# Two cross-attention and expert layers: token lists, maxima in seven pieces, and an opening in order of use

## The chip, the cores and the metric

The kernel runs on one core of one Trainium2 chip. The metric is the device time of one launch in microseconds (us); the median of several runs counts. The profiled execution is one launch taken by the hardware profiler.

A short glossary for the profile: PE is TensorE (matmuls), PEld its weight loads, DVE is VectorE, ACT is ScalarE, POOL is GpSimd, SP is SyncE (here it only issues transfers). L735 is line 735 of the kernel. Every engine works through its own queue of instructions in order and waits on semaphores where data of another engine is needed.

## The reference

Four layers are added to x in turn (4 batches of 512 tokens, 256 wide); ctx_1024 holds 1601 context tokens a batch.

```python
x = x + L0_xattn(ctx_1024, layernorm(x), ...)   # 8 heads of 128, keys: 512 latents + 1601 context
x = x + L0_ffn(layernorm(x), ...)               # 8 experts, top 2, capacity 512 each, tanh gelu
x = x + L1_xattn(ctx_1024, layernorm(x), ...)   # 8 heads of 32, keys: 1601 context
x = x + L1_ffn(layernorm(x), ...)               # 8 experts, top 2, no capacity, exact gelu
```

In the first attention the latents are normalized a second time, queries come from the latents, keys and values from latents and context together, and every score row goes through a softmax over 2113 keys. The last layer is, per token, a softmax over its top two router logits (and ties with the second), and the weighted sum of these experts:

```python
logits = xf @ Wr + br
thresh = lax.top_k(logits, 2)[0][:, 1:2]
weights = softmax(where(logits >= thresh, logits, -inf), axis=-1)
h = gelu(einsum('td,edh->eth', xf, W1) + b1[:, None, :])
out = einsum('etd,te->td', einsum('eth,ehd->etd', h, W2) + b2[:, None, :], weights)
```

## The kernel before

All is float32, in tiles of 128 partitions. A scheduler places the instructions on the engines by the order of the program and by what they depend on; inside a block `in_order` fixes the order of the program on the named engines. The stages follow one another.

**First attention** (lines 529 to 899; profile to about 1640 us). The opening loads x, the constants, the context of batch 0 and the weights (`load_ctx`, 562; the loads stand at 546 to 582), normalizes the context by all 13 tiles at once and the latents twice (`keys_input`, 584), turns both and writes them into `kvin`, whose layout is 17 blocks of 4 x 32 positions (`group`, 607). The output bias is summed by eight matmuls, each with a weight tile that DVE fills (801). `queries_keys` (661) makes one head's queries and keys; each of its five key steps (681) takes 512 neighbouring positions of `kvin`, of all four quarters, so that it needs the whole context. Then 128 steps follow, each one head and 128 queries: `scores` (729) puts 128 x 2113 scores into the single five-bank buffer `ps_s`, DVE takes the maximum (743), ACT the exp (749), and `exchange` (752) moves the result between partitions by 16 transfers, 12 issued by SP and 4 by ACT; one step later DVE turns it (764), and from step 3 on PE weighs the values (772). `attn` has two buffers, so the exp of step n+2 waits for the exchange of step n. Work for later steps is put into `later[n]`.

Before the first step two things are issued: `clear_rows` (370), which fills the DRAM tables `rows_a` (2048 rows) and `rows_b` (18688 rows) of 265 numbers each with an empty row, from SP; and `clear_slots` (178), which clears the slots of the first expert layer, from POOL.

**First expert layer** (to about 1940 us): per expert 512 slots, then the results are gathered again.

**Second attention** (lines 1056 to 1373; 1940 to 2665 us): 16 units (batch, half of the heads, half of the queries) of 13 key tiles. For each unit the row maxima are needed beforehand: `maxima` (1122) is called eight times for the next unit while this one runs; a call makes four matmuls of 400 keys into two buffers of `ps_s` (three buffers of two banks in all, which `weights` shares) and two reductions on DVE (1141). `negated` and `to_row` (1148, 1159) put the negative maximum into an extra row of the queries. `weights` (1173) makes the scores of one key tile and their exp; `add_weights` (1196) sums the exps, on POOL for the tiles in `by_pool`, else on DVE; `weigh` (1204) multiplies with the values. The loop takes two key tiles a step: maxima, two `weights`, further maxima, then sums and weighing of the tiles of the step before. Beside it, at fixed steps, stand routing of the last layer (`route2`, 382) and keys and values of later batches.

`route2` normalizes and routes a batch. It builds `pay`, for each token 256 numbers, its own number as a float, and 8 weights, and POOL scatters these rows to `rows_a` (at most 256 rows an expert from the first three batches) and `rows_b` (the rest), 521.

**Second expert layer** (lines 1379 to 1694): first eight tiles of 256 rows, one for each expert, from `rows_a` (`first_tile`, 1402, SP loads them straight); then 13 tiles from `rows_b` (`further_tile`, 1566: POOL gathers rows and weights). `told` (1388) casts the token's number in a row to an integer, `to`; `turned` (1427), `hidden` (1437) and `second` (1459) compute; `add_out` (1475) adds the result to the output with a POOL scatter by `to`. Rows without a token have the number 65536, which the scatter leaves out.

## Time and profile before

| what | us |
|---|---|
| time, median of 3 runs (3011.76 to 3015.57) | 3014.13 |
| the profiled execution | 3014.63 |
| its span, first to last instruction | 3012.6 |
| mean granted TensorE clock | 0.965 |
| busy: DVE / ACT / POOL | 1444.5 / 931.1 / 473.7 |
| first maximum of the first attention starts | 57.07 |
| L743 maximum (128 of them), each | 2.36 |
| L749 exp (128), each | 2.02 |
| L1141 maxima reduction (256), each | 0.98 |
| L1477 scatter to the output on POOL (42), each | 1.58 |

The 4 MB for the slots and 21.5 MB for the rows are written by the clears: 36 transfers of 530 KB and one of 265 KB to `rows_b`, 4 of 530 KB to `rows_a`, 8 of 512 KB to the slots. The span is read by stretches: where TensorE's busy time equals the stretch and its clock is 1.00, only its own work counts; elsewhere one looks for what it waits for. "Idle before" in a group of instructions is the time in which the engine had nothing to do just before them, with the instruction or transfer that ended it.

### The profile page before, as it was taken

The page shows a single profiled execution, that of the slowest core. Times are in us where ns is not written, and L with a number is a line of the kernel's source. Part 1 is how long each engine was busy: PE and PEld are TensorE (multiplying, and loading weights), DVE is VectorE, ACT ScalarE, POOL GpSimd, SP SyncE. Part 2 cuts the span into 40 slices and gives each one's busy share as a digit, 9 for nine tenths or more (in the row PEclk, how much of TensorE's full clock was granted, in tenths as well). Part 3 has the DMA queues.
Part 4 walks back from the last instruction along what each step waited for, and adds up shares of the span by engine and source line. Part 5 has one row for each costly group of instructions (what it writes and reads, how often), then busy time and mean ns, then how long its engine had stood idle before and what let it go on. Part 6 is the DMA issues. An engine that isn't in the chain of part 4 may idle for free. (4 is left out here: it accounts for less than half of the span.)

```text
span 3012.6 us, 35574 instructions
## 1 busy us (share of the span) xinstructions
PE 2781.7 (92%) x13426; PEld 1846.2 (61%) x13426; DVE 1444.5 (48%) x2324; ACT 931.1 (31%) x1312; POOL 473.7 (16%) x340
## 2 busy tenths in 40 slices
PE   5699999999999999999997999788988888898998
PEld 2466676666666667666665566544444444467887
DVE  4256447554476444464444100177775757751110
ACT  2233234232343333332321212123433434341221
POOL 1000000100001000010000100122424434343442
PEclk9899999999999999999998999889999999999999
DMA  8743334433343333333334233210101110045652
GB/s 297 234 123 94 99 92 105 112 96 92 94 113 104 98 86 95 93 102 97 92 96 148 93 98 105 66 27 14 30 26 36 30 35 22 13 172 165 193 171 73
DMA packets 165103, 295.95 MB, mean 98 GB/s; under 512 B 43287, under 2 KB 81752, under 8 KB 161848
## 3 DMA queue, kind: packets, MB, share of 16 engines
q1 hardware_dynamic: 124024, 204.45, 24.2%
q0 software_dynamic: 16320, 53.42, 5.9%
q10 hardware_dynamic: 24576, 35.68, 4.6%
q8 instruction: 109, 1.79, 0.3%
q14 instruction: 74, 0.61, 0.1%
HBM read 97.86 MB, written 49.76 MB: 49 GB/s over the span
## 5 line engine op out<-in xcount | busy, mean ns | idle before, releaser
L743 DVE TENSOR_REDUCE top<-ps_s 128x1 f32<-128x2113 f32 x128 | 301.8, 2358 | 578.9 <-PE ps_s L735 578.9
L772 PE MATMUL ps_o<-pT,v 128*128 128x256 f32 x2176 | 520.9, 381 | 7.8 <-DVE pT L764 7.8
L735 PE MATMUL ps_s<-kT,qT 128*128 128x512 f32 (+1 forms) x1280 | 489.0, 527 | 26.7 <-ACT attn L749 26.3
L772 PEld LDWEIGHTS ps_o<-pT,v 128*128 128x128 f32 x2176 | 410.9, 191 | 124.8 <-issue 69.9
L735 PEld LDWEIGHTS ps_s<-kT,qT 128*128 128x128 f32 x1280 | 241.5, 191 | 276.3 <-issue 239.9
L749 ACT ACTIVATE attn<-ps_s,top 128x2113 f32<-128x2113 f32 x128 | 258.9, 2023 | 486.1 <-DVE top L743 411.5
L764 DVE STREAM_TRANSPOSE pT<-swapped 128x2176 f32<-128x2176 f32 x128 | 312.4, 2441 | 70.2 <-DMA swapped<-attn 59.4
L1141 DVE TENSOR_REDUCE tops<-ps_s 128x2 f32<-128x800 f32 (+1 forms) x256 | 241.0, 984 | 150.7 <-PE ps_s L1133 150.6
L1180 PE MATMUL ps_w<-asked,keyed 64*128 64x256 f32 (+1 forms) x1664 | 243.7, 418 | 45.7 <-DVE tops L1141 39.4
L685 PE MATMUL ps_k<-kvin,wkv 128*128 128x512 f32 (+1 forms) x640 | 261.9, 533 | 5.2 <-ACT kT L692 5.2
L718 PE MATMUL ps_v<-wkv,kvin 128*128 128x256 f32 x1088 | 253.5, 381 | 0.0
L1202 POOL TENSOR_TENSOR sum<-sum,pT 128x1024 f32<-128x1024 f32 x80 | 197.0, 2463 | 334.4 <-ACT pT L1193 243.5
L1180 PEld LDWEIGHTS ps_w<-asked,keyed 64*128 64x128 f32 (+1 forms) x1664 | 150.4, 193 | 155.6 <-DVE tops L1141 79.7
L1193 ACT ACTIVATE pT<-ps_w 128x1024 f32<-128x1024 f32 (+1 forms) x176 | 178.2, 1023 | 195.4 <-PE ps_w L1180 191.8
L718 PEld LDWEIGHTS ps_v<-wkv,kvin 128*128 128x128 f32 x1088 | 204.9, 190 | 32.7 <-issue 3.4
L692 ACT ACTIVATE kT<-ps_k,bqk 128x512 f32<-128x512 f32 (+1 forms) x160 | 97.1, 620 | 268.1 <-DMA swapped<-attn 128.8
L685 PEld LDWEIGHTS ps_k<-kvin,wkv 128*128 128x128 f32 x640 | 116.5, 192 | 81.0 <-issue 67.1
L1202 DVE TENSOR_TENSOR sum<-sum,pT 128x1024 f32<-128x1024 f32 x96 | 153.3, 1597 | 6.2 <-ACT pT L1193 3.0
L725 ACT COPY v<-ps_v 128x512 f32<-128x512 f32 x144 | 79.8, 560 | 226.2 <-PE ps_v L718 154.0
L1445 PE MATMUL ps_h<-xT,w_e 128*128 128x256 f32 x640 | 143.7, 383 | 3.7 <-issue 3.7
L1133 PE MATMUL ps_s<-kT,qT 32*128 32x400 f32 (+1 forms) x1024 | 142.1, 582 | 3.2 <-ACT pT L1193 2.6
L1464 PE MATMUL ps_y<-w_e,hT 128*128 128x256 f32 x640 | 144.4, 385 | 0.0
(261 smaller groups left out, 2635.6 us busy)
## 6 DMA issues: line engine op xcount, KB each, us to landing
swapped<-attn SPq DMA_DIRECT2D x1536, 68.0 KB
swapped<-attn ACTq DMA_DIRECT2D x512, 68.0 KB
rows_b<-empty SPq DMA_DIRECT2D x36, 530.0 KB
w<-in_w_dram SPq DMA_DIRECT2D x16, 1024.0 KB
w_e<-in_wall_dram SPq DMA_DIRECT2D x7, 2052.0 KB
cT<-in_ctxT_dram SPq DMA_DIRECT2D x4, 1601.0 KB
keyed<-kT SPq DMA_DIRECT2D x32, 200.1 KB
ctx_b<-in_ctx_dram SPq DMA_DIRECT2D x4, 1536.0 KB
```

What stands on the lines that cost most here:

```text
L685: nc.tensor.matmul(ps[:, :n], lhsT=wkv[:, c, hs], rhs=flat_kvin[c][:, j0 : j0 + n], start=c == 0, stop=c == DC - 1,)
L718: nc.tensor.matmul(ps[:, k, :], lhsT=flat_kvin[c][:, j * P : (j + 1) * P], rhs=wkv[:, c, cols], start=c == 0, stop=c == DC - 1,)
L735: nc.tensor.matmul(flat[:, j0 : j0 + n], lhsT=qT[:, t * P : (t + 1) * P], rhs=kT[:, j0 : j0 + n], start=True, stop=True,)
L743: nc.vector.tensor_reduce(top, flat[:, :L], AX.X, ALU.max, negate=True)
L749: nc.scalar.activation(attn[:, :L], flat[:, :L], AF.Exp, bias=top, accum_out=total)
L764: nc.vector.transpose(pT[:, :, k * P : (k + 1) * P].rearrange("p c (a i) -> p a c i", a=4), swapped.rearrange("p a (c i) -> p a c i", i=32),)
L772: nc.tensor.matmul(ps, lhsT=v[:, j - parts[part][0], (h % 2) * DH0 : (h % 2 + 1) * DH0], rhs=pT[:, j, :], start=j == 0, stop=j == NB - 1,)
L1141: nc.vector.tensor_reduce(tops[u][:, t, 2 * pair : 2 * pair + 2, k], pss[pair][:, :, : hi - lo], AX.X, ALU.max,)
L1180: nc.tensor.matmul(ps[:r, s, pair * QH : (pair + 1) * QH], lhsT=keyed[o][64 * s : 64 * s + 64, pair, j * P : j * P + r], rhs=asked[u % 3][ ...
L1193: nc.scalar.activation(pT[:r], ps[:r], AF.Exp)
L1202: (nc.gpsimd if k else nc.vector).tensor_tensor(to, to, pT[:r], ALU.add)
L1464: nc.tensor.matmul(ps, lhsT=hT[:, f, r * P : (r + 1) * P], rhs=w(WB1 + f * D, D), start=f == 0, stop=f == FC - 1,)
```

## The change

Three parts, in one diff.

Token lists: `rows_a` and `rows_b` now hold one row per token in the order of the tokens, written by one plain transfer each for a batch, and one zero row at the end. What is scattered are token numbers of 4 bytes, into `list_a` and `list_b`, which are filled with the number of the zero row at first (`clear_lists`). A tile of the last layer reads its list (`listed`, from SP for the first eight tiles, by a POOL gather for the others), then gathers its rows by it on POOL (`fetched`); the list itself is `to` for the scatter to the output. The slots are cleared by SP, one of eight transfers every second step from step 4 on, out of one zeroed tile.

Opening: loads are issued in an order written out, the context in groups of four tiles, the weights of head 0 before the rest. Context statistics and scaling go by four tiles (`first`), scaling on ACT; latents, statistics, turns, queries and keys of head 0 are interleaved in a fixed order. A key step now takes one quarter of the positions (and a fifth step the last block). The output bias goes to step 13.

Second attention: maxima come in seven pieces, six of 512 keys and one with the last 65 keys of both query tiles; they stand between the two key tiles of a step, and `by_pool` has four tiles in place of six, the first of which only starts POOL's sum.

```diff
-ROWS = E * PLACES
+LIST = E * PLACES
+TA = T - S
...
-    rows_a = dram.tile([E * G, PAY], F32, name="rows_a")
-    rows_b = dram.tile([ROWS + G, PAY], F32, name="rows_b")
-
-    def clear_slots(zeros):
-        for i in range(SLOTS // (4 * P)):
-            nc.gpsimd.dma_start(
-                slot_x[i * 4 * P : (i + 1) * 4 * P, :].rearrange("(p r) d -> p r d", p=P), zeros
+    list_a = dram.tile([E * G, 1], I32, name="list_a")
+    list_b = dram.tile([LIST + G, 1], I32, name="list_b")
+    rows_a = dram.tile([TA + 1, PAY], F32, name="rows_a")
+    rows_b = dram.tile([T + 1, PAY], F32, name="rows_b")
...
+    def clear_slots(zeros, i):
+        tc.keep_in_program_order(
+            nc.sync.dma_start(
+                slot_x[i * 4 * P : (i + 1) * 4 * P, :].rearrange("(p r) d -> p r d", p=P),
+                zeros.unsqueeze(1).to_broadcast([P, 4, D]),
             )
-
-
-    iota_i = const.tile([P, NT, E], I32, name="iota_i")
+        )
...
-    def clear_rows(empty):
-
-        nc.gpsimd.memset(empty, 0.0)
-        nc.gpsimd.memset(empty[:, :, D : D + 1], NOWHERE)
-        for rows in (rows_a, rows_b):
-            n = rows.shape[0]
-            for i in range(0, n, 4 * P):
-                some = rows[i : min(i + 4 * P, n), :]
-                nc.sync.dma_start(
-                    some.rearrange("(p r) d -> p r d", p=P), empty[:, : some.shape[0] // P, :]
-                )
+    def clear_lists(zeros, nobody):
+
+        for rows, of, n in ((rows_a, list_a, TA), (rows_b, list_b, T)):
+            per = of.shape[0] // P
+            nc.gpsimd.memset(nobody[:, :per], n)
+            nc.sync.dma_start(of.rearrange("(p r) o -> p (r o)", p=P), nobody[:, :per])
+            nc.sync.dma_start(rows[n : n + 1, :], zeros)
...
-        for rows, at in ((rows_a, place_a), (rows_b, place_b))[b == B - 1 :]:
+        for rows, of, at in ((rows_a, list_a, place_a), (rows_b, list_b, place_b))[b == B - 1 :]:
+            at0 = (b * NT + first) * P
+            nc.sync.dma_start(
+                rows[at0 : at0 + n * P, :].rearrange("(t p) d -> p t d", p=P), pay
+            )
             for k in range(2):
                 for t in range(n):
                     j = b * NT + first + t
                     nc.gpsimd.indirect_dma_start(
-                        out=rows[:, :],
+                        out=of[:, :],
                         out_offset=bass.IndirectOffsetOnAxis(ap=at[k][:, j : j + 1], axis=0),
-                        in_=pay[:, t, :],
+                        in_=token[:, j : j + 1],
                         in_offset=None,
-                        bounds_check=E * G - 1 if rows is rows_a else ROWS - 1,
+                        bounds_check=E * G - 1 if of is list_a else LIST - 1,
...
+        of_ctx = a["ctx"][0, : (NM - 1) * P, :].rearrange("(t p) d -> p t d", p=P)
+        loading = ExitStack()
+        loading.enter_context(in_order(nc.sync))
+        for n0 in range(0, NM - 1, 4):
+            nc.sync.dma_start(ctx_b[:, n0 : n0 + 4, :], of_ctx[:, n0 : n0 + 4, :])
+            if n0 == 0:
+                load_vectors(gbl, "gamma_lat", "beta_lat")
+                load_vectors(bqk, "bq", "bk", "bv")
+                nc.sync.dma_start(wq[:, :, :DH0], of_wq[:, :, :DH0])
+                nc.sync.dma_start(wkv[:, :, :DH0], of_wkv[:, :, :DH0])
+                load_vectors(gbm, "gamma_media", "beta_media")
+        nc.sync.dma_start(ctx_b[:TAIL, NM - 1, :], a["ctx"][0, (NM - 1) * P :, :])
+        nc.sync.dma_start(wkv[:, :, INNER:], of_wkv[:, :, INNER:])
+        nc.sync.dma_start(wq[:, :, DH0:], of_wq[:, :, DH0:])
+        nc.sync.dma_start(wkv[:, :, DH0:INNER], of_wkv[:, :, DH0:INNER])
...
+                mv, rs = ln_scale(two, mv, 4)
+                away = two.tile([P, 4], F32, tag="nt4", name="away")
+                nc.vector.scalar_tensor_tensor(away, mv[:, :, 0], -1.0, rs, ALU.mult, ALU.mult)
+                for i in range(n):
+                    r = rows_of(n0 + i, NM, TAIL)
+                    of = ctx_b[:r, n0 + i, :]
+                    nc.scalar.activation(
+                        of, of, AF.Identity, scale=rs[:r, i : i + 1], bias=away[:r, i : i + 1]
+                    )
...
-                        rhs=flat_kvin[c][:, j0 : j0 + n],
+                        rhs=kvin[:, c, : NB - 1, k, :] if k < 4 else kvin[:, c, NB - 1, :, :],
...
+        stats, turns = context[::2], context[1::2]
+        for s in (
+            latent[:2] + stats[:1] + latent[2:] + fill[:2] + stats[1:2] + turns[:1] + stats[2:3]
+            + turns[1:2] + fill[2:3] + stats[3:] + turns[2:3] + fill[3:4] + turns[3:] + fill[4:]
...
+        scrap = one.tile([P, NT, D], F32, tag="lat", name="scrap")
+        nc.gpsimd.memset(scrap, 0.0)
+        empty = scrap[:, :2, :].rearrange("p t d -> p (t d)")
+        nobody = one.tile([P, (LIST + G) // P], I32, tag="v1", name="nobody")
+        with in_order(nc.sync):
+            clear_lists(empty[0:1, :PAY], nobody)
+            load_second()
...
+        for i in range(SLOTS // (4 * P)):
+            later[4 + 2 * i].append(lambda i=i: clear_slots(empty[:, :D], i))
+        later[13].append(output_bias)
...
-        edges = [k * M // HG for k in range(HG + 1)]
+
+        rest = M // 512 * 512
+        pieces = [[(t, j0, 512)] for t in range(2) for j0 in range(0, rest, 512)]
+        pieces.append([(t, rest, M - rest) for t in range(2)])
+        assert 2 * (M - rest) <= 512
+        n_tops = rest // 512 + 1
...
+            for t, j0, n in pieces[g]:
+                q0 = f * QH + t * P
+                for i in range(HG):
+                    rows = slice(i * DH1, (i + 1) * DH1)
+                    nc.tensor.matmul(
+                        pss[i // 2][:, i % 2, at : at + n],
+                        lhsT=qTs[b][rows, o, q0 : q0 + P],
+                        rhs=kvs[b][0][o][rows, j0 : j0 + n],
+                        start=True,
+                        stop=True,
+                    )
+                at += n
+            t, j0, n = pieces[g][0]
...
-        by_pool = (1, 3, 5, 7, 9, 11)
+        by_pool = (1, 4, 7, 10)
...
-                step = NM * u - 5 - NM + (g * NM) // (2 * HG)
+            for g in range(len(pieces)):
+                step = NM * u - 6 - NM + 2 * g
...
-            first, *more = ahead.pop(step // 2, [None])
-            if first:
-                maxima(*first)
+
             fresh = []
             for k in range(step, step + 2):
                 u, j = divmod(k, NM)
                 if u < n_units:
                     fresh.append((u, j, weights(u, j)))
-            for g in more:
-                maxima(*g)
...
-        def told(rows, share_of):
-
-            to = five.tile([P, GR], I32, tag="to", name="to")
-            share = five.tile([P, GR], F32, tag="share", name="share")
-            for r in range(GR):
-                nc.vector.tensor_copy(to[:, r : r + 1], rows[r][:, D : D + 1])
-                share_of(share[:, r : r + 1], rows[r][:, D + 1 :])
-            return rows, to, share
...
+        def listed(k, pool):
+
+            to = pool.tile([P, GR], I32, tag="to", name="to")
+            if k < E:
+                of = list_a[k * G : (k + 1) * G, :].rearrange("(p r) o -> p (r o)", p=P)
+                nc.sync.dma_start(to, of)
+                return to
+            for r in range(GR):
+                nc.gpsimd.indirect_dma_start(
+                    out=to[:, r : r + 1],
+                    out_offset=None,
+                    in_=list_b[:, :],
+                    in_offset=bass.IndirectOffsetOnAxis(
+                        ap=state["x_idx"][:, r, k - E : k - E + 1], axis=0
+                    ),
+                    bounds_check=LIST + G - 1,
+                    oob_is_err=False,
+                )
+            return to
...
+        def fetched(k, to, three=three, four=four):
+
+            of, n = (rows_a, TA) if k < E else (rows_b, T)
             rows = []
...
                 got = three.tile([P, PAY], F32, tag=f"rows{r}", name=f"rows{r}")
-                nc.sync.dma_start(got, rows_a[e * G + r * P : e * G + (r + 1) * P, :])
+                nc.gpsimd.indirect_dma_start(
+                    out=got,
+                    out_offset=None,
+                    in_=of[:, :],
+                    in_offset=bass.IndirectOffsetOnAxis(ap=to[:, r : r + 1], axis=0),
+                    bounds_check=n,
+                    oob_is_err=False,
+                )
                 rows.append(got)
-            if e == 0:
+            if k == 0:
                 w2 = one.tile([P, WIDE - WB1], F32, name="w2_first")
...
+            if k + 2 <= n_tiles:
+                pools = (three, four) if k + 2 < n_tiles else (spare, spare)
+                tiles.append(fetched(k + 2, lists[k + 2], *pools))
+            if k + 3 <= n_tiles:
+                lists.append(listed(k + 3, seven if k + 3 < n_tiles else spare))
+            if k + 1 < n_tiles:
+                here = ready(*tiles[k + 1])
```

## The prediction

> **What bounds the kernel now.** I read the page's summary and its 40 slices first, then the busy time by stretch, and then the waits inside the stretches that are not full.
>
> ```profile
> PE 2781.7 (92%) x13426; PEld 1846.2 (61%) x13426; DVE 1444.5 (48%) x2324; ACT 931.1 (31%) x1312; POOL 473.7 (16%) x340
> ...
> PE   5699999999999999999997999788988888898998
> ...
> PEclk9899999999999999999998999889999999999999
> DMA  8743334433343333333334233210101110045652
> GB/s 297 234 123 94 99 92 105 112 96 92 94 113 104 98 86 95 93 102 97 92 96 148 93 98 105 66 27 14 30 26 36 30 35 22 13 172 165 193 171 73
> ```
>
> TensorE is busy 92% of a span of 3012.6 us (PE row). Its digits are 9 in the first attention, 7 to 9 in the second, with holes at the start and in between. DMA and GB/s are at their highest in slices 1 and 2, where PE is at its lowest.
>
> ```profile
> 54.00:130.00 76.00, 47.53 (x142) 27.51 (x141) 15.95 (x12) 17.64 (x24) 0.00 (x0) 0.83 0.86 307
> ...
> 200.00:1600.00 1400.00, 1398.90 (x5253) 951.64 (x5252) 734.56 (x940) 457.98 (x628) 41.28 (x48) 1.00 0.39 99
> ...
> 1985.00:2665.00 680.00, 588.63 (x4978) 314.64 (x4974) 481.33 (x756) 277.62 (x332) 276.38 (x148) 0.94 0.10 26
> ...
> 2665.00:2745.00 80.00, 64.99 (x329) 53.14 (x328) 28.80 (x127) 21.17 (x43) 21.88 (x17) 0.88 0.56 193
> ```
>
> (Columns: stretch, its us, then busy us and instructions of PE, PE's weight loads, DVE, ACT, POOL; the granted clock; DMA share; GB/s.) From 200 to 1600 PE is full at clock 1.00: nothing but less PE work helps there. From 54 to 130 it is idle 76.0 - 47.5 = 28.5 us and, at clock 0.83, loses 47.5 x 0.17 = 8.1 more. The second attention (1985 to 2665) has 680 - 588.6 = 91.4 idle and 588.6 x 0.06 = 35 lost to the clock, with DVE at 481/680 = 71%. The second expert stage opens (2665 to 2745) with 15.0 idle. After 2745 PE is full again.
>
> Why 54 to 130 is empty, by the timeline (start, us, engine, line):
>
> ```profile
> 48.94 53.16 SPq L378 DMA_DIRECT2D rows_b<-empty  x30
> ...
> 100.05 8.52 ACTq L756 DMA_DIRECT2D swapped<-attn  x4
> ...
> 102.20 26.90 SPq L756 DMA_DIRECT2D swapped<-attn  x34
> ...
> 115.61 2.44 DVE L764 STREAM_TRANSPOSE pT<-swapped 128x2176 f32<-128x2176 f32 x1 [32.30 <-DMA swapped<-attn]
> ...
> 115.66 2.02 ACT L749 ACTIVATE attn<-ps_s,top 128x2113 f32<-128x2113 f32 x1 [19.31 <-DMA swapped<-attn]
> ...
> 117.82 5.63 PE L735 MATMUL ps_s<-kT,qT 128*128 128x512 f32 x10 [18.66 <-ACT attn L749]
> ```
>
> SP issues row clears from 49 to 102 us, and the first exchange (swapped<-attn) gets its twelve SP transfers only at 102.20. ACT's third exp, at 115.66, overwrites the buffer that this exchange reads and waits for it, and PE's next scores at 117.82 wait for the exp. This is one chain: clears, exchange, ACT, PE.
>
> In the second attention the rows and the PE waits (us in total, times, longest) are:
>
> ```profile
> L1202 POOL TENSOR_TENSOR sum<-sum,pT 128x1024 f32<-128x1024 f32 x80 | 197.0, 2463 | 334.4 <-ACT pT L1193 243.5
> ...
> L1202 DVE TENSOR_TENSOR sum<-sum,pT 128x1024 f32<-128x1024 f32 x96 | 153.3, 1597 | 6.2 <-ACT pT L1193 3.0
> ...
> L1141 DVE TENSOR_REDUCE tops<-ps_s 128x2 f32<-128x800 f32 (+1 forms) x256 | 241.0, 984 | 150.7 <-PE ps_s L1133 150.6
> ```
> ```profile
> PE ps_w L1180 <- DVE tops L1141: 39.4, 33, 4.9
> ...
> PE ps_c L468 <- DVE earlier L464: 16.7, 3, 5.6
> ...
> PE ps_r L1163 <- DVE shift L1150: 15.2, 8, 3.0
> ```
>
> DVE is the engine that PE waits for: 39.4 us because a maximum has not freed a score buffer, 15.2 for the last maximum of a unit, 16.7 inside routing. DVE's add takes 1597 ns here although the timeline has undisturbed ones of 1.21 us.
>
> At the start of the second expert stage:
>
> ```profile
> DVE to L1395 <- DMA out_dram<-y,to: 32.5, 2, 16.8
> ```
> ```profile
> PE ps_x L1504 <- DVE xT L1434: 8.1, 1, 8.1
> ```
>
> DVE's cast of a row's destination (to) sits 32.5 us in two waits for an older result's scatter to release its buffer; behind it in DVE's queue is the copy xT, and PE waits 8.1 us for that.
>
> **What the Trainium skill says.** "SBUF — State Buffer", Who interferes with whom: DVE and GpSimd share a port pair under an exclusive lock, so a DVE instruction with two SBUF inputs blocks against a GpSimd one that reads SBUF. The trace agrees: DVE adds of 1.21 us alone and 2.3 to 3.1 us beside a POOL add. "TensorE: Matmul & The Clock Gate", What's actually happening: the PE clock halves after an idle window of about 3.4 us. The trace shows 0.50 to 0.88 for some 15 us after the 8.1 us gap. "DMA: Bandwidth & Descriptors", Issuing engines are not separate DMA queues: transfers of all queues share the 16 engines. The trace agrees: among the clears, at a DMA share of 1.02, ACT's four transfers of 65.60 hold ACT up as well (9.93 us before its next kT).
>
> **Part 1, token lists instead of cleared rows.** Removed: 36 x 530 KB + 265 KB + 4 x 530 KB = 21.5 MB of clears, 54 us at the 397 GB/s of the 90 to 100 us stretch, and their 41 issues on SP. Added: two list clears (8 and 75 KB) and two zero rows. The slot clears (8 x 512 KB, from POOL) become one SP issue every second step from step 4: about 1 us in front of 12 exchange issues of 0.55 us, in a step of 12.1 us, 1.3 us of transfer; hidden by PE, which is full; if that cover failed, 8 x 1 us. What stays of the hole 54 to 130: steps 0 to 3 have no weighing to fill PE, the loop is scores 3.9, maximum 2.36, exp 2.2, so about 8.5 us a step, against some 10 us of PE work a step (four scores 15, queries and keys 9.4, values 15); and the changed order puts the next batch's layer norm on DVE (some 9.5 us, then 5 us) between these maxima, which delays two of them by about 3 us each. I keep 5.5 us of the 28.5 + 8.1: gain 31 (bounds 20 and 35).
>
> In the second attention each batch's 8 or 16 scatters stay, of 4 bytes a row instead of 1060: the trace has no such scatter. POOL's issue is the same form (995 ns); the landing is between the same (about 2.8 us from one to the next) and somewhat less: taken at nothing, as POOL is not waited for there. Two straight stores per batch are added on SP, idle there.
>
> In the second expert stage the rows of a tile come by list: SP loads list_a (first 8 tiles) or POOL gathers two columns of list_b, then POOL gathers two row tiles. POOL per tile: 2 scatters x 1.58 + weights 1.04 + rows 2 x 1.03 + lists 2 x 1.03 = 8.3 us of the 14.3 us that a tile takes on PE (2764.62 to 2778.95), fetched two and three tiles ahead: hidden. At the start it is not: before, rows were loaded at 2649, 23 us ahead of use. Now the lists' pool waits for the previous stage's engines, then a load of about 2 us, a POOL issue of 1.03 and a landing of 2.4 (the wait for rows_a in the trace) follow before the first transpose: +7 us idle, +1.5 us clock. Bounds +2 (pools free early) and +14 (POOL still behind the scatters of batch 2). Gone: the cast of to, so PE's 8.1 and 3.0 us of idle and the clock after it (3.63 x 0.27 + 5 x 0.08 + 4.98 x 0.50 + 5 x 0.12 = 4.5): -15.6. Next late there is POOL's queue, which has slack of some 20 us for tiles 3 to 7. Net -7 (bounds -14 and +8).
>
> **Part 2, the opening.** Before, the first maximum starts at 57.07. Changed: x lands at about 5.3 us (98 GB/s over the first 5.5 us is 0.54 MB); two layer norms of the latents on DVE, 5.5 each (4 pairs of 0.6, chain 1.7, apply 1.4); then, strictly in order, four groups of stats (2.4), root and chain (1.7), apply on ACT (4 x 0.37, from a 128x256 ACT copy of 370 ns), half the evacuation on DVE (1.0) and half on ACT (1.0), keys and their evacuation (1.7 + 0.7). DVE waits for PE's queries and for ACT's roots behind a kT evacuation. Adding along it I come to 24.5 for the queries, 35 for the second group, 43 for the third, 49 for the last keys and 52.5 for the first maximum: -5 (bounds 0 and -14). The output bias (8 x 0.70 us of matmuls, each waiting for a DVE copy) leaves this chain, where PE was idle, and enters step 13, where PE is full: 16 instructions of 7.07/32 = 0.22, 3.5 us, plus round trips behind DVE's 2.4 us transposes: +7 (bounds +3 and +12). The whole first attention: -31 - 5 + 7 = -29.
>
> **Part 3, maxima.** Per unit DVE now does 16 x 0.984 = 15.7 us of maxima and 6 adds x 1.60 = 9.6. Changed: 12 maxima of 1024, 0.984 + 224/0.96 ns = 1.22 us, and 2 of 260, 0.42: 15.5; 8 adds, as POOL keeps 3 of its 5. An add lies between 1.21 (never blocked) and 1.60 (as now); POOL's adds fall to 0.6, so the excess of 0.39 becomes about 0.25: 1.46, in all 11.7. DVE +1.9 us a unit, 30 us in all. PE's work is equal: 24 matmuls of 512 columns and 8 of 65 against 32 of 400. What changes is where they stand. Before, with three score buffers, maxima stood ahead of both key tiles, and the second tile needed the first maximum's buffer 1.0 us after its scores, just the time of one maximum: every late DVE add stopped PE. Now it stands between the tiles; the maxima's buffers are wanted 2.1 and 3.1 us later, and take 1.2 and 2.4. So 0.7 us of slack, one piece in each step instead of up to two, while DVE's load per step (2.4 + 1.8) comes near PE's 4.3. I take half of the 39.4 away, 5 of the 15.2, leave the other 37 us: -25 idle. With idle at 10% instead of 13% of the stretch I scale the clock's 35 us to 22: -13. Sum -38. Bounds: -85 (both waits and most of the clock loss gone), +20 (32 more adds x 1.46 = 47 on PE's path, less 27).
>
> **Sum.** -29 - 7 - 38 = -74 against a span of 3012.6; the execution took 3014.63, 2.0 more than its span, 0.5 above the median of 3014.13. So 3014.1 - 74 = 2940, and I take 2938.
>
> **Rivals.** (a) DVE becomes the bound of the second attention: for it, 80% load and its in-order queue; against, the slack above. Part 3 gives 0 to +20: 3014 - 36 + 10 = 2988. (b) The slack removes nearly all DVE waits and the clock stays up: -85: 2893; for it, the 144 us that DVE itself waits for scores; against, routing and closing also load DVE. (c) The clears were not what held the first exchange (SP's order or ACT's table loads do): the 31 us stay: 2969. Against it is the timeline above. (d) Slower: in the second expert stage, gathers of list and rows in series behind scatters on POOL miss their tile. It decides once a tile takes over 14.3 + 74/21 = 17.8 us; at 5 us for each of 21 tiles, +105: 3045. Against: 6 us of slack per tile and a lead of two tiles.
>
> **Chances.** Forecast 0.60, (a) 0.15, (b) 0.13, (c) 0.08, (d) 0.04. The forecast's own bounds reach 2910 to 2968; adding (a) and most of (b) gives 2890 to 2985. About 0.2%, 6 us, is what can be told from no change: faster 0.95, same 0.01, slower 0.04.
>
> **What would show it.** No long SP run after 49 us, the third exp near 73 us, PE full from about 95; first maximum at 50 to 55; the second attention about 640 us long, DVE near 80%, its adds near 1.46 us; no wait of to on out_dram; a PE gap of 5 to 10 us where the experts start. Wrong would be: exchanges still late, a DVE over 85% busy with more waits of PE on tops, or tiles longer than 14.3 us after the eighth.

## The result and the profile after

The changed kernel takes 3003.19 us (median of 7 runs, 2997.82 to 3005.18) against 3013.52 of the kernel before (7 runs): a ratio of 0.9965, 95% interval 0.9953 to 0.9976. That is 10 us less; 74 less were forecast. (One of the four executions of a kernel shown below, with 64-byte entries and late weights, took 3897 us where the others took 2967 to 2969; its ratio leaves that one out.) The profiled execution took 3004.21 us with a span of 3002.5. Of its page, the summary, TensorE's slices and those of the transfer engines:

```profile
PE 2782.1 (93%) x13426; PEld 1841.7 (61%) x13426; DVE 1451.9 (48%) x2275; ACT 941.4 (31%) x1330; POOL 439.9 (15%) x346
...
PE   6999999999999999999996999688989898867998
...
DMA  5444343444433443343433332200110100055553
```

TensorE's first two slices were 5 and 6 and are 6 and 9; the transfer engines' first two fell from 8 and 7 to 5 and 4. But near the end of PE's row, where a 9 and an 8 stood, there are now a 6 and a 7 (slices of 75 us; these are the 36th and 37th, from 2627 to 2777 us). To see where the time went I cut both traces at the same five events: the start of the last weighing of the first attention (ps_o<-pT,v), of the last result copy of the first expert stage, of the first and the last TensorE work of the second attention's tiles (ps_w; ps_n<-sum), and of the last scaled result y. The lengths are read from the two profiled executions:

| stretch | before, us | after, us | difference | forecast |
|---|---|---|---|---|
| first attention, from the span's start | 1634.9 | 1600.0 | -34.9 | -29 |
| first expert stage | 303.3 | 303.7 | +0.4 | 0 |
| to the first tile of the second attention | 47.2 | 48.0 | +0.8 | 0 |
| second attention | 686.7 | 669.4 | -17.3 | -38 |
| second expert stage | 327.3 | 366.9 | +39.6 | -7 |
| from the last y to the span's end | 13.2 | 14.5 | +1.3 | 0 |

So the first attention gained what it should, and the second less than half of what it should; the second expert stage, which should have gained 7 us, lost 39.6. The busy times by stretch of the changed kernel, columns as before:

```profile
54.00:130.00 76.00, 73.31 (x256) 47.11 (x255) 44.70 (x81) 29.97 (x41) 0.00 (x0) 0.98 0.43 106
...
1951.00:2621.00 670.00, 593.82 (x5027) 312.33 (x5030) 498.98 (x752) 281.75 (x335) 208.20 (x117) 0.94 0.10 28
2621.00:2661.00 40.00, 11.91 (x51) 9.15 (x44) 6.25 (x25) 5.40 (x10) 10.99 (x11) 0.56 0.60 187
2661.00:2721.00 60.00, 43.61 (x203) 37.06 (x202) 11.37 (x57) 12.64 (x27) 18.85 (x17) 0.83 0.44 102
...
2781.00:2981.00 200.00, 200.00 (x953) 176.06 (x952) 27.17 (x86) 46.95 (x112) 101.31 (x84) 1.00 0.53 163
```

54 to 130 is now filled: 2.7 us idle against 28.5. The second attention is 76.2 us short of full (670 - 593.8) against 95.3 before (687 us with 591.7 busy), at the same mean clock of 0.94. After it come 40 us with TensorE busy for 11.9 and 60 us with 43.6, at clocks of 0.56 and 0.83. From 2781 on tiles follow each other without a gap, as forecast. The loss is thus in the opening of the stage alone, and TensorE's waits in it (us in total, times, longest) name it:

```profile
PE tp L1545 <- DMA rows<-rows_a,to: 27.3, 2, 25.5
PE ps_h L1557 <- issue: 12.7, 1, 12.7
```

The second row's cause isn't named there. At that place, from 2702 to 2714 us, DVE's copies of the sixth tile's shares (the expert's weights of its rows) wait for its rows, the last 10.0 us for the second half of them. xT of the fourth tile, which TensorE needs, stands behind them in DVE's queue: it runs at 2713.88, though its transposes were done at 2695.

```profile
2694.41 0.60 PE L1545 MATMUL tp<-ident,rows 128*128 128x128 f32 x4
...
2702.88 1.04 POOL L1495 DMA_INDIRECT rows<-rows_a,to  x1 [0.30 <-issue]
...
2713.81 0.15 DVE L1531 COPY share<-rows 128x1 f32<-128x1 f32 x1 [10.01 <-DMA rows<-rows_a,to]
2713.88 0.68 DVE L1546 COPY xT<-tp 128x512 f32<-128x512 f32 x1
```

So both are waits for rows that POOL gathers by list. How the first comes about, by the timeline:

```profile
2623.26 0.99 POOL L529 DMA_INDIRECT list_b<-token,place_b  x1 [2.67 <-DMA list_b<-token,place_b]
...
2625.85 0.81 SPq L1515 DMA_DIRECT2D w_e<-in_wall_dram  x2
...
2629.05 0.98 POOL L529 DMA_INDIRECT list_b<-token,place_b  x1 [4.80 <-DMA list_b<-token,place_b]
...
2638.49 0.98 POOL L529 DMA_INDIRECT list_b<-token,place_b  x1 [8.47 <-DMA w_e<-in_wall_dram]
2639.78 1.05 POOL L1495 DMA_INDIRECT rows<-rows_a,to  x1 [0.31 <-issue]
...
2649.02 0.47 PE L1545 MATMUL tp<-ident,rows 128*128 128x128 f32 x1 [25.53 <-DMA rows<-rows_a,to]
```

POOL's queue holds the last three scatters of the third batch's numbers into list_b, and each waits until the one before has landed: 4.8 us of waiting at 2629.05, and 8.5 at 2638.49, which the trace puts down to the three loads of 2 MB of weights that SP issued from 2625.85 on. The row gathers for the first tile stand behind them in the same queue, start at 2639.78, and the first transpose comes at 2649.02, 28 us after the second attention's last sums.

### The profile page after: what moved, and what is told of

It reads as the page before. It is cut to its first block, busy times and chain, and to the rows that moved or that the text cites. A ratio compares the mean times of both kernels' runs of the same rounds, so it can differ in the third digit from the quotient of the medians.

```text
span 3002.5 us, 35538 instructions
## 1 busy us (share of the span) xinstructions
PE 2782.1 (93%) x13426; PEld 1841.7 (61%) x13426; DVE 1451.9 (48%) x2275; ACT 941.4 (31%) x1330; POOL 439.9 (15%) x346
## 5 line engine op out<-in xcount | busy, mean ns | idle before, releaser
L819 DVE STREAM_TRANSPOSE pT<-swapped 128x2176 f32<-128x2176 f32 x128 | 312.4, 2441 | 35.8 <-DMA swapped<-attn 26.0
L1218 DVE TENSOR_REDUCE tops<-ps_s 128x2 f32<-128x1024 f32 (+1 forms) x224 | 237.4, 1104 | 138.8 <-PE ps_s L1207 138.4
L1279 DVE TENSOR_TENSOR sum<-sum,pT 128x1024 f32<-128x1024 f32 (+1 forms) x128 | 179.5, 1403 | 11.8 <-ACT pT L1270 5.7
L1279 POOL TENSOR_TENSOR sum<-sum,pT 128x1024 f32<-128x1024 f32 x48 | 124.5, 2594 | 329.8 <-ACT pT L1270 329.5
L1557 PE MATMUL ps_h<-xT,w_e 128*128 128x256 f32 x640 | 143.6, 383 | 12.7 <-issue 12.7
L1207 PE MATMUL ps_s<-kT,qT 32*128 32x512 f32 (+1 forms) x1024 | 140.2, 580 | 12.0 <-ACT kT L1005 6.5
```

The lines of the kernel that those rows point to most:

```text
L819: nc.vector.transpose(pT[:, :, k * P : (k + 1) * P].rearrange("p c (a i) -> p a c i", a=4), swapped.rearrange("p a (c i) -> p a c i", i=32),)
L1218: nc.vector.tensor_reduce(tops[u][:, t : t + at // n, 2 * pair : 2 * pair + 2, j0 // 512], of, AX.X, ALU.max,)
L1279: (nc.gpsimd if k else nc.vector).tensor_tensor(to, to, pT[:r], ALU.add)
L1557: nc.tensor.matmul(ps[:, f, :], lhsT=w(at, P), rhs=xT[:, c, :], start=c == 0, stop=c == DC - 1,)
```

## Which theories were tried

Theory: the lists cost the second expert stage its 40 us, and three things are in it: scatters of 4 bytes that land slowly, weights on the transfer engines ahead of the rows, and the longer way from list to rows itself. Rivals: the stage is longer because it starts earlier and colder; or the queue's length alone does it, whatever a scatter takes. For the second attention: either the clock or DVE's load kept the rest of the gain away.

## Experiments on the loss

**Rows in place again.** The changed kernel with the old form of scatter and loads; the clears of the places one every second step of the first attention:

```diff
-                        out=of[:, :],
+                        out=rows[:, :],
...
-                        in_=token[:, j : j + 1],
+                        in_=pay[:, t, :],
...
+        for i, some in enumerate(clear_rows()):
+            later[20 + 2 * i].append(lambda some=some: clear_some(some))
```

> The changed kernel with the rows themselves scattered to their experts' places again, as in the kernel before (1060 bytes a row, straight loads of the first eight tiles' rows, no lists), and the clears of those places spread as one transfer every second step over the first attention. Theory L (the lists cost the second expert stage some 40 us: 366.9 against 327.3 us from the last sum of the second attention to the last result): the stage goes back to 325 to 335 us, the first and second attention keep their gains of 35 and 17, total 2955 to 2972. Rival (the stage is longer for another reason, such as an earlier and colder start): the stage stays near 365, total 2995 to 3010.

Measured: 2990.8 us (ratio 0.9922, interval 0.9905 to 0.9938). The second expert stage is back at 330.7 us and the second attention at 672.8, as the theory wants. The total missed the interval because the first attention took 1619.0 us, 19 more than with lists. The stage begins 19 us later here, too, so that an early start is ruled out in full only by the next run, in which it begins at 2620 us, as in the changed kernel (2621).

**The same, with the clears elsewhere.** Six to an expert in the first expert stage:

```diff
-            later[20 + 2 * i].append(lambda some=some: clear_some(some))
...
                 w_next = expert_weights(wexp, "w1", "w2", e + 1)
+                for _ in range(6):
+                    for some in clears:
+                        clear_some(some)
+                        break
```

> The kernel with rows scattered in place (as rows_back: new opening, new maxima, no lists), but the 41 clears stand six to an expert in the first expert stage instead of one every second step of the first attention. In rows_back the first attention took 19 us more than in the changed kernel. If these are the clears among the exchanges of that stage: the first attention ends near 1600 again, and the total is 2966 to 2975. If the 19 us come from the rest (another packing of the first stage): the first attention still ends near 1619, total 2985 to 2995. If clears hold up the experts' weights: the first expert stage grows from 303 to 315 or more.

Measured: 2970.01 us (0.9855, 0.9839 to 0.9872); first attention 1600.0, first expert stage 303.9, second 331.1. So the 19 us were the 41 clears among the exchanges of the first attention, and the early start is not the cause of the loss. In the first expert stage the same 21.5 MB cost nothing: it takes 303.7 us without them and 303.9 with them, at a share of the transfer engines of 0.31 without and 0.67 with. The lists weren't needed to fill the opening's hole; the clears only had to stand elsewhere.

**The lists alone.** The first part of the change on the kernel before:

```diff
-        clear_rows(empty)
-        clear_slots(empty[:, :, :D])
+            clear_lists(empty[0:1, :PAY], nobody)
...
+            later[4 + 2 * i].append(lambda i=i: clear_slots(empty[:, :D], i))
```

> The kernel before with the first part of the change alone (token lists, no cleared rows, slot clears spread); old opening and old maxima. The forecast's step for the first attention: 29 to 32 us less there from the clears alone, with the opening's own 2 us (5 less 7) missing. If the second expert stage loses its 40 us to the lists: total 3014 - 31 + 40 = 3023 (3015 to 3030), slower than before. If the loss needs the earlier end of the second attention or the new maxima: 2980 to 2990.

Measured: 3016.71 us (1.0011, 1.0004 to 1.0018), a little slower than before. The first attention ends at 1602.6, 32.3 earlier, as expected. The second expert stage takes 360.4 (+33.1), a little less than the 40 expected, and the second attention, with the old maxima, 692.3 (+5.6). TensorE's waits at the end of it and in the second expert stage:

```profile
PE tp L1483 <- DMA rows<-rows_a,to: 18.6, 2, 16.2
...
PE ps_n L1243 <- POOL sum L1215: 10.4, 1, 10.4
```

The last row belongs to the end of the second attention: TensorE waits 10.4 us for POOL's last sums (1.6 before). With six key tiles of thirteen on POOL, the list scatters in its queue hold up its adds as well.

**Do small scatters land late?** 30 scatters on POOL in the first attention, where it has nothing else to do:

```diff
+            with in_order(nc.gpsimd):
+                for width in (1, 16, 64, 128, 256):
+                    probe(width)
```

> The changed kernel with 30 more scatters on POOL in the first attention, to places that nobody reads, six each of 4, 64, 256, 512 and 1024 bytes a row, each waiting for the one before of its size. Theory S (a scatter of 4 bytes a row lands later than one of a kilobyte): from one issue to the next 4.5 to 5.5 us at 4 bytes and 2.8 to 3.3 at 1024. Rival (the landing doesn't depend on the bytes and the lists' intervals came from what else was under way): equal within 0.5 us for all sizes. Total within 5 us of the changed kernel, as POOL has nothing else to do there.

Measured, in one execution: at 4 bytes a row 7.7 to 10.6 us from one issue to the next, far over the 4.5 to 5.5 expected; at 64 bytes 2.5 to 4.2, after a first one of 7.6 with the last 4-byte scatter still under way; at 256 bytes and more 2.4 to 3.4, and one of 4.6. The size seems to matter, but between 4 and 64 bytes only. And the total of 3026.61 missed its bound of 5 us: the first attention ended 15.5 us later. In the 20 us from 240 on TensorE was busy for 10.8: with the probe's scatters under way the transfers moved 69 GB/s at a share of 0.78, against 135 GB/s at 0.53 in the changed kernel. The engines were thus busy longer for fewer bytes: such a scatter is dear for others too. How much, these windows don't settle: in the 20 us before it was 96 against 124 GB/s, in the 20 us after 113 against 100.

**Size, or neighbours?** The 4-byte places of the first probe lie side by side, so that 128 rows share 512 bytes. Now 4 bytes with 64 bytes from place to place, then 64, 16 and 4 bytes side by side, six each:

```diff
+        nc.gpsimd.iota(apart, pattern=[[16 * P, NX]], base=0, channel_multiplier=16)
...
+                probe("apart", 1, apart, 16 * T)
+                probe("w16", 16, token, T)
+                probe("w4", 4, token, T)
+                probe("w1", 1, token, T)
```

> 24 more scatters in the first attention, six each: 4 bytes to places 64 bytes apart, then 64, 16 and 4 bytes to neighbouring places. Theory S (size): 4 bytes are as slow apart as side by side, 7 us or more from one to the next, 16 bytes between. Rival N (neighbours: 128 writes into the same 512 bytes get in each other's way): 4 bytes apart take 2.5 to 4 us like 64 bytes, and only the side-by-side ones are slow.

The timeline of it (start, duration, and in brackets POOL's wait for the scatter before), one or two rows of each group in this order:

```profile
222.53 1.01 POOL L899 DMA_INDIRECT probe_apart<-x,apart  x1 [1.42 <-DMA probe_apart<-x,apart]
225.69 0.98 POOL L899 DMA_INDIRECT probe_apart<-x,apart  x1 [2.15 <-DMA probe_apart<-x,apart]
...
239.23 0.98 POOL L899 DMA_INDIRECT probe_w<-x,token  x1 [1.77 <-DMA probe_w<-x,token]
...
253.45 0.98 POOL L899 DMA_INDIRECT probe_w<-x,token  x1 [1.40 <-DMA probe_w<-x,token]
...
273.49 0.98 POOL L899 DMA_INDIRECT probe_w<-x,token  x1 [7.07 <-DMA probe_w<-x,token]
282.31 0.98 POOL L899 DMA_INDIRECT probe_w<-x,token  x1 [7.85 <-DMA probe_w<-x,token]
```

Apart, 4 bytes land nearly as fast as the others: POOL waits 1.4 to 3.4 us, at 64 bytes 1.5 to 1.8 and at 16 bytes 1.4 to 1.8. Side by side it waits 7.1 to 8.0 us. The slow group stands last here and stood first in the other probe, so its place in the row isn't the reason. The theory of size fell; it is 4-byte writes to neighbouring places. This kernel took 3020.11 us, and its first attention ended 7.6 us later than the changed kernel's. The Trainium skill, "DMA: Bandwidth & Descriptors", Specifications, gives 512 bytes as the size below which a transfer is done as read-modify-write; no step at 512 bytes is to be seen in these intervals (2.4 to 3.4 us at 256, 512 and 1024 bytes, but for one of 4.6), nor between 16 and 64 bytes side by side. What happens between the writes inside the memory no trace shows.

**List entries of 64 bytes.** The changed kernel with each token's number sixteen times, so that no two entries share 64 bytes:

```diff
-    list_b = dram.tile([LIST + G, 1], I32, name="list_b")
+    list_b = dram.tile([LIST + G, WL], I32, name="list_b")
...
-                        in_=token[:, j : j + 1],
+                        in_=token16[:, j, :],
```

> The changed kernel with every list entry 64 bytes wide (the token's number sixteen times) instead of 4, in the scatters, the clear and the reads; the chain of operations is the same. Theory S (the scatters of 4 bytes a row are what is dear: 7.7 to 10.6 us from one to the next in the first attention against 2.5 to 3.3 at 256 bytes and more): intervals of the list scatters fall from 4 to 6 us to about 3, the first tile's rows land some 20 us earlier, and the second expert stage falls from 367 to 335 to 350 us; total 2970 to 2987. Rival Q (the chain list, rows, scatters in POOL's one queue is too long whatever the bytes): the stage stays at 358 or more, total 2995 to 3005.

Measured: 2975.62 us (0.9872, 0.9856 to 0.9889). The second expert stage takes 342.4 us, 24.5 less, with the same chain of operations; this and the total lie in the intervals of theory S. The second attention is unchanged (670.3). The opening of the stage:

```profile
2620.77 0.98 POOL L537 DMA_INDIRECT list_b<-token,place_b  x1 [4.52 <-DMA list_b<-token,place_b]
...
2623.16 0.98 POOL L537 DMA_INDIRECT list_b<-token,place_b  x1 [1.41 <-DMA list_b<-token,place_b]
...
2624.87 1.05 POOL L1504 DMA_INDIRECT rows<-rows_a,to  x1 [0.73 <-DVE t L145]
...
2633.03 0.18 PEld L1554 LDWEIGHTS tp<-ident,rows 128*128 128x128 f32 x1 [11.67 <-DMA rows<-rows_a,to]
```

The last scatter now waits 1.4 us. The gathers start 15 us earlier, 6 us after the second attention's last sums instead of 19, and TensorE's first wait is 11.6 us instead of 25.5. Rival Q is out for this part. As 16 bytes side by side were quick too, entries of 64 bytes may be wider than needed; narrower ones were not tried.

**Weights behind the rows**, with 4-byte entries and with 64-byte ones:

```diff
-                if k < E:
+                if k < 4:
+                    nc.sync.dma_start(landed[k - 1 : k, :], rows[GR - 1][:1, :1])
+                    tc.keep_in_program_order(
+                        nc.sync.dma_start(t, a["wall"][k * P : (k + 1) * P, :])
+                    )
+                elif k < E:
```

> The changed kernel, but the weights of the tiles 1 to 3 of the second expert stage are loaded only after the rows of the same tile have landed (a load behind a one-word store on SP that reads the rows). Theory W (6.2 MB of weights on the transfer engines hold up the last list scatter by some 8.5 us and the row gathers behind it): TensorE's first wait for rows falls from 25.5 to 14 to 17 us, total 2990 to 2996. Theory Q (POOL's in-order chain of list scatters, each waiting for the one before, is the delay by itself): the wait stays above 22 us, total 3000 to 3008; more if the weights are then late in turn.

> List entries of 64 bytes and, besides, the weights of tiles 1 to 3 loaded only behind the rows of their tile. With 64 bytes alone the stage takes 342.4 us and TensorE still waits 11.6 us for the first rows. If the weights among the last scatters and gathers make that rest: the wait falls to 4 to 7 us, stage 333 to 338, total 2966 to 2972. If it is the way list, rows, landing itself: no change, 2973 to 2980; if the later weights are then waited for, over 2980.

Measured with 4 bytes: 3002.2 us (0.9956, 0.9941 to 0.9971), no different from the changed kernel, so that theory W missed its total and theory Q its wait. TensorE's waits in the opening:

```profile
PE tp L1551 <- DMA rows<-rows_a,to: 17.8, 1, 17.8
PE ps_x L1622 <- DVE xT L1552: 17.1, 1, 17.1
```

The first wait fell from 25.5 to 17.8 us, but the later one grew from 12.7 to 17.1: the last four scatters of the fourth batch follow each other at 6.5, 4.3 and 8.0 us in front of the next row gathers, and DVE's xT waits behind the shares that need those. The stage is 6.6 us shorter at 360.3; the second attention of that execution was longer (678.2 against 669.4), which no run explains. With 64 bytes: 2968.35 us (0.9847, 0.9827 to 0.9867), stage 334.6, first wait 6.5, as expected. In the stage the weights are worth 6.6 us with slow scatters and 7.8 with quick ones; in the total only the latter shows.

**The cast's wait alone.** The forecast priced the wait of to on out_dram at 15.6 us in the kernel before. Here it is taken out of the kernel with rows in place and its clears in the first expert stage:

```diff
-            to = five.tile([P, GR], I32, tag="to", name="to")
+            to = nine.tile([P, GR], I32, tag="to", name="to")
```

> The kernel with rows in place and clears in the first expert stage (2970 us), with nine buffers instead of five for the rows' destinations (to), so that DVE's cast no longer waits for the result scatter of five tiles earlier. The forecast priced that wait at 15.6 us (11.1 idle and 4.5 of clock) in the kernel before; in this one TensorE waits 15 us in the same place. If the wait is the limit there: the second expert stage falls from 331 to 314 to 321, total 2953 to 2961. If POOL's chain of result and row scatters is next late: 322 to 329, total 2961 to 2968.

Measured: 2960.09 us (0.9821, 0.9804 to 0.9837), the fastest of all runs and some 43 us below the changed kernel; stage 321.1 against 331.1. TensorE's waits in the stage of the kernel with five buffers

```profile
PE ps_h L1524 <- issue: 11.3, 2, 9.9
PE ps_x L1583 <- DVE xT L1513: 3.8, 1, 3.8
```

and with nine:

```profile
PE ps_y L1544 <- DVE y L1571: 7.6, 1, 7.6
```

15.1 us of waiting are gone, and 7.6 stand in their place where y waits. The wait was worth 10.0 us in this kernel, at the low edge of what was expected, and not 15.6.

## Experiments on the second attention

**The maxima alone.** The third part of the change on the kernel before:

```diff
-        edges = [k * M // HG for k in range(HG + 1)]
+        pieces = [[(t, j0, 512)] for t in range(2) for j0 in range(0, rest, 512)]
+        pieces.append([(t, rest, M - rest) for t in range(2)])
...
-        by_pool = (1, 3, 5, 7, 9, 11)
+        by_pool = (1, 4, 7, 10)
```

> The kernel before with the third part of the change alone (maxima in seven pieces between key tiles, four key tiles to POOL); rows, clears and opening as before. If the part is worth what the traces of the two kernels say, 17 us: 2994 to 2999. If slow list scatters on POOL ate a part of its gain in the changed kernel, and it is worth the forecast's 38 by itself: 2974 to 2982. If the gain in the second attention came from elsewhere: over 3005.

Measured: 2996.06 us (0.9944, 0.9927 to 0.9960): the second attention takes 670.7, so the part is worth 16 us by itself. The lists take nothing from it in the changed kernel, whose second attention takes 669.4.

**Its two halves.** The new order with POOL's six key tiles, and the old order with POOL's four:

```diff
-        by_pool = (1, 4, 7, 10)
+        by_pool = (1, 3, 5, 7, 9, 11)
```

> The kernel before with the maxima in seven pieces between key tiles, but POOL keeping its six key tiles of thirteen (five adds a unit, not three). If DVE's load is what the new order leaves as the bound of the second attention, giving 32 adds back to POOL shortens it further: 670.7 to 650 to 662, total 2975 to 2988. If POOL's adds slow DVE's by the shared port as much as they relieve it: 668 to 675, total 2993 to 3001. If POOL then falls behind: over 680.

> The kernel before with one edit: POOL takes four key tiles of thirteen instead of six, so that DVE has 32 adds more; maxima as before. Of the 16 us that the third part gives alone, the same part with POOL's six gave some 11. If fewer POOL adds help DVE in the old order too: second attention 680 to 684, total 3006 to 3011. If DVE is the bound of the old order and only the new places of the maxima make room: 690 to 710, total 3018 to 3036.

Measured: new order with six 2999.94 us (0.9948, 0.9931 to 0.9964), stage 675.8 in an execution 6 us over the median; so giving DVE's adds back to POOL shortens nothing. Old order with four 3051.25 us (1.0128, 1.0111 to 1.0145), stage 718.8, the case of DVE as the bound, and beyond the 710 and 3036 expected for it. One of TensorE's waits in the latter:

```profile
PE ps_w L1180 <- DVE tops L1141: 65.6, 42, 5.4
```

In the old order 32 more adds on DVE cost 32 us, most of it in waits on maxima (65.6 against 39.4); in the new order they cost nothing that can be told (3000 and 2996 us, with overlapping intervals). So DVE's load held up the old order, and at this size it doesn't hold up the new one. Whether the seven pieces or their places between the key tiles do it was not tried apart.

## Why the forecast was wrong, step by step

**Clears (-31).** Right in size, and in cause as far as was tried: the lists alone ended the first attention 32.3 us earlier. The clears of the slots were spread in the same edit and not tried by themselves.

**Opening (-5 + 7).** The first maximum starts at 50.28 us, 6.8 earlier, and the changed kernel's first attention ends 2.6 before that of the lists alone: -2.6 instead of +2.

**Maxima (-38).** The mechanism was right: DVE's add takes 1.40 us (1.46 forecast) and the wait on maxima fell further than assumed. A large maximum takes 1.216 us (1.22 forecast; the two reductions of the kernel before, 983 ns for 800 elements and 2358 for 2113, give 1.05 ns an element, and so 1.22 for 1024). TensorE's waits in the second attention of the changed kernel:

```profile
PE ps_r L1240 <- DVE shift L1227: 16.7, 7, 4.4
PE ps_w L1257 <- DVE tops L1218: 9.5, 6, 4.1
```

39.4 became 9.5, not 20. The size was off in two terms. The wait for the unit's last maximum (shift) was to fall from 15.2 to 10 and is 16.7; with small new waits on ACT's exps (6.3 and 3.6 us, where 0.9 and 2.6 stood) the idle time fell by 19 us instead of 25. And the clock's share of 13 didn't come: the mean clock stayed at 0.94 with less idle time, and TensorE was busy for 593.8 us, not less than the 591.7 before. That is the 17.3 us measured: 19 less idle and 2 more busy. Scaling the clock's loss with idle time was the part of this step without a measurement behind it, and in proportion (10% for 13%) it would have made 27 us of the 35, a gain of 8 and not of 13. What keeps the clock there with less idle time wasn't tried.

**Second expert stage (-7).** Here the forecast failed, by 47 us, in two sentences. The first is "the landing is between the same (about 2.8 us from one to the next) and somewhat less: taken at nothing, as POOL is not waited for there." Where one list scatter follows another in POOL's queue, 2.4 to 5.8 us lie between them, mostly over 4, and 9.4 up to 2638.49 among the weights, where 2.8 or less was assumed; and in the changed kernel POOL is waited for, because the row gathers stand behind the scatters in its queue. The second is the start of the stage, "+7 us idle, +1.5 us clock", bounded by 14 for "POOL still behind the scatters of batch 2" (the third batch): the case named was the one that happened, but 14 was too little for it, as the first wait alone is 25.5 us. The forecast names neither slow scatters nor weights ahead of the rows there. The forecast's "slack of some 20 us for tiles 3 to 7" was used up in the same way by the fourth batch's scatters. The measured sum is: 10.0 gained from the cast, and 45.8 lost to the lists (366.9 - 321.1, the same kernel but for the lists and the place of the clears), of which 24.5 go with 64-byte entries and 7.8 more with weights behind rows (342.4 - 334.6). 13.5 us remain (334.6 - 321.1). No run takes them apart; they are presumably the way from list to rows itself, which the forecast put at 8.5. With rows in place and the cast's wait left in, the stage lay between 325.6 and 331.1 us in six kernels, so these terms are good to some 5 us; 45.8 less 10.0 is 35.8, where 39.6 was measured.

**The rivals.** (d) had the right queue and the right stage, gathers on POOL behind scatters, but as a cost of every tile; it comes in the opening of the stage only, and from 2781 us on TensorE is full. At some 46 us it cost less than the 105 assumed there and was enough to eat the gain of the other parts. (c) fell with the lists alone; (a) and (b) fell with the halves of the third part: 32 adds more or less on DVE don't move the new order, so it isn't the bound; and the waits on maxima are mostly gone, yet the stage shortens by 16 and not by 85, as other waits on DVE stay (shift 16.7, and 17 in routing) and the clock doesn't rise.

The three parts would thus have been worth most of the forecast without the lists: with rows in place, clears elsewhere and nine buffers the kernel takes 2960.09 us, 53 less than before. The 21 us still missing are in the second attention, which falls 24 us short of its forecast, while the first gains 7 more than forecast.

## What to carry to other kernels

When data on a path is made smaller, price the transfers anew: issue and landing need not fall with the bytes, and a scatter of single words to neighbouring places can land later than whole rows. A queue that nobody waited for before is on the path once the next stage's first loads are put into it, so list what stands ahead of them there, each with its wait. Work that fills the transfer engines in a critical opening may only need another place: moved to a stage with room, it cost nothing.

## What was unexpected of the hardware

A 128-row scatter of 4 bytes a row to neighbouring places takes 7.7 to 10.6 us from one to the next, against 2.4 to 4.4 with the places 64 bytes apart and 2.4 to 2.8 with neighbouring rows of 16 bytes; and while such scatters are under way, other transfers are slowed: 69 against 135 GB/s in the same 20 us of the first attention, and in the second probe 62 against 91 in the 20 us from 280 on. 41 clears of 530 KB, one every second step of some 12 us, cost a stage with a mean transfer share of 0.4 another 19 us, though TensorE shows only 10.5 us of waits between 100 and 1500 us. Over the whole stage it is also busy for longer, 1569.7 us against 1561.3 of the changed kernel, with a mean clock of 0.97 in the two stretches of 100 us with the longest waits (from 500 and from 900), where it is full at 1.00 in the changed kernel.
